# First pointwise layer by Strassen's scheme, with a ring of image blocks and a convolution by pairs of outputs

## The chip, the cores and the metric

The kernel runs on one core of a Trainium2 chip. The metric is the device time of one execution in microseconds (us). All arithmetic is fp32.

## What is computed

Two layers work on an image of 4 x 64 x 64 pixels with 256 channels. Layer 0 is full attention over the 4096 pixels of each image, added to its input. Layer 1 is a 3 x 3 depthwise convolution with three outputs per channel, two pointwise layers with a GELU between them, a residual, and attention over each pixel's 3 x 3 neighbours.

```python
# layer 0, x: (4, 4096, 256)
q, k, v = x @ Wq + bq, x @ Wk + bk, x @ Wv + bv        # q, k: 32 channels, v: 256
attn = softmax(einsum('bnd,bmd->bnm', q, k))
h = gamma * einsum('bnm,bmc->bnc', attn, v) + x
# layer 1
perceived = depthwise_conv3x3(h, w_perc) + b_perc       # 768 channels, zero padding
hid = gelu(einsum('bphw,dp->bdhw', perceived, w_up1) + b_up1)   # 768 -> 512
h_new = h + einsum('bdhw,cd->bchw', hid, w_up2) + b_up2         # 512 -> 256
q, k, v = split(einsum('bhwc,dc->bhwd', h_new, w_qkv) + b_qkv, 3)
w = softmax over 9 neighbours of (q . k_neighbour) / 16
return h_new + sum over 9 neighbours of w * v_neighbour
```

## The kernel before

Channels lie on the 128 partitions, in two halves of 128. The pixels of the four images are cut into 32 blocks of 512 pixels (8 rows). The main loop (L801) has one **slot** per block and a slot has 16 **points** (L800). In slot s the attention of layer 0 is computed for block s, and beside it layer 1 for earlier blocks: the convolution of block s-2, the two pointwise layers, scores and values of block k = s-3, and the result of the neighbour attention of block a = s-5. All orders are written out by hand: what a point issues goes to each engine's queue in that order, and each engine works through its queue in order.

At a point the kernel issues, in this order:

- at even points `energy` (L281): four matmuls that fill the four banks of tile `e` in PSUM for the next group of keys, and at every point `weight` (L293), the exponential on ScalarE of half of `e` into one of three `p` buffers;
- the jobs of that point, from the list at L807: `hidden` (L450, first pointwise layer, one of four output tiles of 128 channels), `update` (L475, second pointwise layer), `guide`, `scores`, `local_values` (L612), `local_product` (L741);
- `product` (L298): eight 512-column records on the two `acc` banks;
- `add_up` (L312), on VectorE, which sums the weights in `den`;
- some of the slot's convolution steps (`perceive`, L400): 48 steps spread evenly over 14 points. A step is one tap of one output tile of 128 x 512, `perc = window * weight + perc` on VectorE (L428). Tap 0 runs on ScalarE (L424). An output's eight steps follow one another before the next output's begin.

At the end of a slot, `partial_sums` and `finish` (L353) close the attention: a small matmul `dps` (L360), a reciprocal, a copy and a transpose, two scalings of the `acc` banks into `o` (L372), and two additions into the image `xp` in SBUF (L377), all on VectorE. GpSimd then adds every `o` into a watch tile (`watch`, L171, L176).

PSUM has eight banks: four for `e`, two tagged "acc", two tagged "m". All jobs and `dps` take the two "m" banks in turn (`job_bank`, L103), so a job's first matmul waits until whoever reads the result of the job two before it has done so.

`hidden(s, d)` multiplies six weight tiles of 128 x 128 by the six `perc` tiles of 512 columns into one bank, and ScalarE applies GELU with the bias out of the bank:

```python
for i in range(NPC):                                   # NPC = 6
    nc.tensor.matmul(ps, lhsT=wup1[:, i, bass.ts(d, P)], rhs=percs[s][i], ...)
nc.scalar.activation(hids[s][:, d, :], ps, AF.Gelu, bias=bup1[:, d : d + 1])
```

In the last slot of an image (slots 7, 15, 23) the queries, keys and values of the next image are projected (`fetch`, `project_qk`, `project_v`); in slot 0 those of blocks 3 to 7 of the first image are. `project_v` (L243) moves values out of PSUM on VectorE with an added bias. `xp` holds a whole padded image; `renew` (L113) brings its blocks over SP's DMA queue, the first image's eight at the start, later ones one per slot. SP's queue also carries the `ka`, `packed` and `qa` transfers and the outputs.

After the loop (from L897) a tail closes blocks 28 to 31. Its PSUM has six banks for jobs. Tail and last slot (L829) have job lists of their own; the last slot also runs most of the convolution of block 30.

Of the kernel before, what the change touches and what calls it, by code (L numbers as in the profile page):

```python
# [9 lines left out]
F32 = mybir.dt.float32  # L10
# [30 lines left out]
NSLOT = B * NBLK  # L41

# [8 lines left out]
def attention_then_perception_kernel(  # L51
# [34 lines left out]
    def unshifted():  # L86
# [23 lines left out]
        xp = pool.tile([P, CH, HP * WP], F32, tag="xp", name="xp")  # L110
        xv = xp.rearrange("p c (h w) -> p c h w", w=WP)

        def renew(slot, cs=slice(0, CH)):  # L113
            b, g = divmod(slot, NBLK)
            at = slice((1 + g * RB) * WP, (1 + (g + 1) * RB) * WP)
            nc.sync.dma_start(out=xp[:, cs, at], in_=x[b, :, cs, at])
# [8 lines left out]
        bv = loaded(b_v.partition_broadcast(P), "bv", [P, C], nc.scalar)  # L125
# [11 lines left out]
        for c in range(CH):  # L137
            nc.gpsimd.memset(xp[:, c, 0:WP], 0.0)
            nc.gpsimd.memset(xp[:, c, (HP - 1) * WP :], 0.0)
# [42 lines left out]
        def fetch(s):  # L182
# [18 lines left out]
            at = slice(1 + g * RB, 1 + (g + 1) * RB)  # L201
            for c in range(CH):
                to = staged[s][:, c, :].rearrange("p (h w) -> p h w", w=W)
                if b > 0:
                    nc.sync.dma_start(out=to, in_=rows[:, c, at, 1 : 1 + W])
                elif c == 0:
                    nc.vector.tensor_copy(to, xv[:, c, at, 1 : 1 + W])
                else:
                    nc.scalar.copy(to, xv[:, c, at, 1 : 1 + W])

        def project_qk(s):
# [17 lines left out]
            for r in range(2):  # L229
                at = 2 * r * CQK  # L230
                keys[s + r] = tile_of([P, P], "ka", f"ka_{s + r}", NBLK + 2)
# [11 lines left out]
        def project_v(s, pair, tag="m"):  # L243
# [4 lines left out]
            for i in range(2):  # L248
# [6 lines left out]
            nc.vector.tensor_tensor(  # L255
                values[s][:, 2 * pair : 2 * pair + 2, :],
                ps.rearrange("p (t c) -> p t c", c=C),
                bv.unsqueeze(1).to_broadcast([P, 2, C]),
                ALU.add,
# [93 lines left out]
        def finish(s, parts=((0, RB),)):  # L353

            g = s % NBLK
# [8 lines left out]
            rden = tile_of([P, NB], "rden", f"rden_{s}", 2)  # L364
            on_all(inverse[:, 0, :], turneds[s][:, 0, :], rden)
            watch(inverse.rearrange("p i j -> p (i j)")[:, :n])
            sums.pop(s)
            os = [tile_of([P, NB], "o", f"o_{s}_{c}", 3) for c in range(CH)]
            for r0, r1 in parts:
# [5 lines left out]
                for c, o in enumerate(os):  # L375
                    dst = xv[:, c, 1 + g * RB + r0 : 1 + g * RB + r1, 1 : 1 + W]
                    nc.vector.tensor_tensor(  # L377
                        dst, o[:, n].rearrange("p (h w) -> p h w", w=W), dst, ALU.add
                    )
                if len(parts) > 1:  # L380
                    yield
            for o in os:
                watch(o)
            yield

        def local_denominator(s):
            at = s + LAG_ATT - 1
            lrdens[s] = tile_of([P, NB], "rden", f"lrden_{s}", 2)
# [3 lines left out]
        percs, hids, hs = {}, {}, {}  # L392
        NPERC = NPC + 3
# [6 lines left out]
        def perceive(s, parts):  # L400

            g = s % NBLK
            ahead = s >= NSLOT - LAG_PERC
            percs.setdefault(s, {})

            def begin(i):
                if not ahead:
                    perc = tile_of([P, NB], "perc", f"perc_{s}_{i}", NPERC)
                else:
# [3 lines left out]
                    perc = percs[s, i - i % 2][:, i % 2, :]  # L413
                percs[s][i] = perc
                tap_of(i, 0, 0, RB)

            def tap_of(i, tap, r0, r1):
# [3 lines left out]
                win = xv[:, half, g * RB + dy + r0 : g * RB + dy + r1, dx : dx + W]  # L421
# [8 lines left out]
            for i, taps, r0, r1 in parts:  # L430
                if taps[0] == 0:
                    if i not in percs[s]:
                        begin(i)
                    if ahead and i + 1 < NPC:
                        begin(i + 1)
                for tap in taps:
                    if tap > 0:
                        tap_of(i, tap, r0, r1)
                        yield

        whole = [(i, range(TAPS), 0, RB) for i in range(NPC)]
# [3 lines left out]
            part for i in range(NPC)  # L445
            for part in ((i, range(LOW), 0, RB), (i, range(LOW, TAPS), 0, RB - 1))
        ]
        lower = [(i, range(LOW, TAPS), RB - 1, RB) for i in range(NPC)]
# [26 lines left out]
        def update(s, c):  # L475
            g = s % NBLK
# [8 lines left out]
            for half in range(2):  # L485
# [5 lines left out]
                    xv[:, c, 1 + g * RB : 1 + (g + 1) * RB, 1 + cols.start : 1 + cols.stop],  # L491
# [11 lines left out]
        def combine_steps():  # L503

            names, ws, turned = ("wq", "wk"), [], []
            for i, name in enumerate(names):
                w = tile_of([P, CH, C], "perc", f"{name}_in", NPERC)
# [3 lines left out]
            for name, w in zip(names, ws):  # L511
                t = tile_of([P, CH, C], "perc", f"{name}_turned", NPERC)
# [99 lines left out]
        def local_values(s, t):  # L612
# [8 lines left out]
            for half in range(2):  # L621
                if s < NSLOT - 2:
                    lvs[s, t, half] = tile_of([P, C], "lv", f"lv_{s}_{t}_{half}", 8)
                else:
                    if not half:
                        late[s, t] = tile_of([P, NB], "perc", f"lv_{s}_{t}", NPERC)
# [20 lines left out]
        def scores(s, half):  # L647
# [19 lines left out]
            else:  # L667

                if s < NSLOT:
                    late[s] = tile_of([P, NB], "perc", f"lp_{s}_{half}", NPERC)  # L670
# [61 lines left out]
        def local_reciprocal(s):  # L732
# [4 lines left out]
            lrdens[s] = tile_of([P, NB], "rden", f"lrden_{s}", 2)  # L737
# [3 lines left out]
        def local_product(s, c):  # L741
# [11 lines left out]
            o = tile_of([P, NB], "o", f"lo_{s}_{c}", 3)  # L753
# [22 lines left out]
        for i in range(4, NBLK):  # L776
            renew(i)
# [10 lines left out]
        gam = loaded(gamma.partition_broadcast(P), "gam", [P, 1])  # L788
        wlv = pool.tile([P, CH, C], F32, tag="wlv", name="wlv")
# [11 lines left out]
        for slot in range(NSLOT):  # L801
            b, g = divmod(slot, NBLK)
            if b > 0:
                renew(slot)
# [3 lines left out]
                job(hidden, k, 0) + job(hidden, k, 1), job(local_denominator, a),  # L808
                job(hidden, k, 2), job(local_product, a, 0), job(hidden, k, 3),
                job(local_product, a, 1), job(update, k, 0), job(update, k, 1), [],  # L810
                job(guide, k, 0), job(guide, k, 1), job(scores, k, 0),
                job(scores, k, 1) + job(local_sum, k - 1), job(local_values, k, 0),
                job(local_values, k, 1), [],
# [10 lines left out]
            conv = perceive(slot - LAG_PERC, whole) if slot >= LAG_PERC else iter(())  # L824
            n_steps, stepped = NPC * (TAPS - 1), 0
            if slot == NSLOT - 1:
# [3 lines left out]
                    job(hidden, k, 0) + job(hidden, k, 1), job(local_denominator, a),  # L830
                    job(hidden, k, 2), job(local_product, a, 0) + job(hidden, k, 3),
# [3 lines left out]
                    job(scores, k, 0) + job(hidden, k + 1, 0),  # L835
                    job(scores, k, 1) + job(local_sum, k - 1) + job(hidden, k + 1, 1),
                    job(hidden, k + 1, 2) + job(local_total, a + 1)
                    + job(local_reciprocal, a + 1),
                    job(hidden, k + 1, 3), job(update, k + 1, 0) + job(border, k),
# [6 lines left out]
            for point in range(points):  # L846
# [24 lines left out]
                while stepped < min(n_steps, -(-(point + 1) * n_steps // (points - 2))):  # L871
                    next(conv, None)
                    stepped += 1
                if slot == 0 and point == NG:
# [7 lines left out]
                    wup2 = loaded(w_up2, "wup2")  # L882
                    bup2 = loaded(b_up2, "bup2")
# [75 lines left out]
        return wv, bv, gam, wperc, bperc, wup1, bup1, wup2, bup2, blqk, blv  # L959


    def shifted():
# [16 lines left out]
        nc.scalar.dma_start(out=wqk, in_=w_qk)  # L979
        wqkv = own.tile([P, CH, 3 * C], F32, tag="wqkv", name="wqkv")  # L980
# [373 lines left out]
```

## Time and profile before

| quantity | value |
|---|---|
| median of 3 runs | 3572.64 us (3572.56 to 3573.12) |
| the profiled execution | 3573.02 us |
| its span, first to last instruction | 3571.3 us |
| TensorE busy | 3548.8 us (99%) |
| VectorE / ScalarE / GpSimd busy | 2320.2 / 1113.0 / 612.6 us |
| granted TensorE clock | 0.998 |
| first pointwise layer, L455 | 1536 matmul records, 686.8 us |
| convolution steps on VectorE, L428 | 1554, 1257.5 us |
| a slot without projections (2109.9 to 2215.8) | 105.9 us |

The profiled execution's time is the one that sums are made against; it lies 0.4 us over the median. PE stands for TensorE's matmuls, PEld for its weight loads, DVE for VectorE, ACT for ScalarE, POOL for GpSimd, SP for the engine whose queue issues most transfers. Each fp32 matmul appears as two records.

### The profile page before, as it was taken

Reading aid. Unit: us, or ns where it says so; the run is one execution under the profiler, and the core shown is the slowest. Engines: PE = TensorE matmul, PEld = TensorE weight load, DVE = VectorE, ACT = ScalarE, POOL = GpSimd, SP = SyncE. Lnnn points to the kernel's source line nnn. Section 1 sums busy time; section 2 is a strip of 40 time slices with the busy share of each in tenths; the row PEclk is TensorE's granted clock in tenths of the full one; section 3 lists DMA queues with packets and bytes.
Section 4 is the critical chain, followed back from the end, with each engine's and each line's share of the span. In section 5 each row is a group of like instructions: output and inputs, shape, how many; then the busy total and the mean of one; then the engine's idle time right before and its main releaser. Section 6 shows DMA issues by size and latency. Waiting matters only on the chain.

```text
span 3571.3 us, 29494 instructions
## 1 busy us (share of the span) xinstructions
PE 3548.8 (99%) x11346; PEld 1701.1 (48%) x11346; DVE 2320.2 (65%) x2938; ACT 1113.0 (31%) x1270; POOL 612.6 (17%) x804
## 2 busy tenths in 40 slices
PE   9999999999999999999999999999999999999998
PEld 4444444454444444455444444445544444444445
DVE  3386566657666666665666666665666666666875
ACT  2233333323333333322333333332233333333431
POOL 1000011111121121121111211111121122121123
PEclk9999999999999999999999999999999999999999
DMA  3000000110000000011000000001100000000000
GB/s 105 7 4 3 0 9 15 24 45 15 15 13 6 12 15 15 21 27 42 16 15 15 3 12 15 15 21 36 33 15 15 15 15 3 13 15 15 6 6 25
DMA packets 84533, 64.68 MB, mean 18 GB/s; under 512 B 57280, under 2 KB 62528, under 8 KB 84256
## 3 DMA queue, kind: packets, MB, share of 16 engines
q1 hardware_dynamic: 83568, 62.19, 6.2%
q8 instruction: 91, 1.49, 0.2%
q10 hardware_dynamic: 816, 0.53, 0.0%
q14 instruction: 58, 0.48, 0.0%
HBM read 41.52 MB, written 18.81 MB: 17 GB/s over the span
## 4 chain that ended last, share of the span: by engine, by line
PE 97%; DVE 2%; issue 0%; ACT 0%; DMA 0%; SPq 0%; ACTq 0%; DVEq 0%
PE acc L306 49%; PE hid L455 19%; PE e L287 8%; PE dx L481 6%; PE v L250 3%; PE lv L616 3%; PE g L564 3%; PE lo L747 3%; PE s L657 3%; DVE perc L428 2%; PE qk L216 1%; PE c L596 0%; DVE den L320 0%; PE ld L727 0%; PE dps L360 0%
## 5 line engine op out<-in xcount | busy, mean ns | idle before, releaser
L306 PE MATMUL acc<-p,v 128*128 128x512 f32 x4096 | 1834.2, 594 | 0.3 <-DVE o L372 0.3
L428 DVE SCALAR_TENSOR_TENSOR perc<-xp,wperc,perc 128x512 f32<-128x512 f32 (+1 forms) x1554 | 1257.5, 810 | 525.9 <-ACT perc L424 490.7
L306 PEld LDWEIGHTS acc<-p,v 128*128 128x128 f32 x4096 | 768.3, 190 | 916.0 <-issue 911.2
L295 ACT ACTIVATE p<-e 128x1024 f32<-128x1024 f32 x512 | 524.7, 1025 | 1467.2 <-PE e L287 835.2
L455 PE MATMUL hid<-perc,wup 128*128 128x512 f32 x1536 | 686.8, 600 | 0.0
L320 DVE TENSOR_TENSOR den<-den,p 128x1024 f32<-128x1024 f32 x480 | 594.8, 1239 | 42.8 <-ACT p L295 39.2
L455 PEld LDWEIGHTS hid<-perc,wup 128*128 128x128 f32 x1536 | 285.1, 190 | 389.7 <-issue 382.3
L176 POOL TENSOR_TENSOR watched<-watched,lo 128x256 f32<-128x256 f32 x124 | 157.0, 1266 | 999.0 <-DVE lo L754 994.0
L287 PE MATMUL e<-qa,ka 32*128 32x512 f32 x2048 | 291.9, 640 | 0.0
L481 PE MATMUL dx<-hid,wup 128*128 128x512 f32 x512 | 233.0, 598 | 0.0
L459 ACT ACTIVATE hid<-hid,bup 128x512 f32<-128x512 f32 x128 | 88.1, 688 | 436.3 <-PE hid L455 436.3
L629 DVE TENSOR_TENSOR lv<-lv,blv 128x256 f32<-128x256 f32 x130 | 49.1, 420 | 211.9 <-PE lv L616 211.9
L681 POOL TENSOR_TENSOR lp<-lp,near 128x396 f32<-128x396 f32 x60 | 57.7, 962 | 711.5 <-ACT lp L677 711.5
L487 DVE SCALAR_TENSOR_TENSOR h<-dx,bup,xp 128x256 f32<-128x256 f32 x128 | 56.0, 480 | 165.2 <-PE dx L481 165.2
L481 PEld LDWEIGHTS dx<-hid,wup 128*128 128x128 f32 x512 | 94.6, 190 | 129.9 <-issue 123.9
L424 ACT ACTIVATE perc<-xp,bperc,wperc 128x512 f32<-128x512 f32 x192 | 154.1, 804 | 5.2 <-PE hid L455 5.2
L295 ACT ACT_TABLE_LOAD x91 | 116.8, 1283 | 119.9 <-issue 119.3
L287 PEld LDWEIGHTS e<-qa,ka 32*128 32x128 f32 x2048 | 80.0, 182 | 148.0 <-issue 144.2
L176 POOL TENSOR_TENSOR watched<-watched,o 128x256 f32<-128x256 f32 x128 | 124.0, 969 | 56.2 <-DVE o L372 48.6
L616 PE MATMUL lv<-wlv,h 128*128 128x256 f32 x520 | 126.5, 385 | 1.4 <-DVE lv L629 0.7
L250 PE MATMUL v<-wv,xc 128*128 128x256 f32 x512 | 118.4, 384 | 6.3 <-DMA wv<-in_w_v 5.5
L564 PE MATMUL g<-h,wg 128*128 128x512 f32 x256 | 123.1, 604 | 0.0
(108 smaller groups left out, 1735.3 us busy)
## 6 DMA issues: line engine op xcount, KB each, us to landing
xp<-in_x SPq DMA_DIRECT2D x30, 528.0 KB, 4.2
out<-lo SPq DMA_DIRECT2D x58, 256.0 KB, 2.0
xc<-in_x SPq DMA_DIRECT2D x48, 256.0 KB, 3.4
qa<-packed SPq DMA_DIRECT2D x124, 64.0 KB, 2.1
ka<-st SPq DMA_DIRECT2D x124, 16.0 KB, 1.8
packed<-st SPq DMA_DIRECT2D x31, 64.0 KB, 1.9
wup<-in_w_up SPq DMA_DIRECT2D x1, 1536.0 KB, 7.0
out<-res SPq DMA_DIRECT2D x6, 256.0 KB, 2.0
```

The lines of the kernel that those rows point to most:

```text
L176: nc.gpsimd.tensor_tensor(at, at, values[:, i : min(n, i + C)], ALU.add)
L250: nc.tensor.matmul(ps[:, i * C : (i + 1) * C], lhsT=xc[:, kin, bass.ts(2 * pair + i, P)], rhs=wv[:, kin, :], start=(kin == 0), stop=(kin = ...
L287: nc.tensor.matmul(e[:, j, :], lhsT=key[rows, :], rhs=queries[s][rows, :], start=True, stop=True,)
L295: nc.scalar.activation(p, energies[s, G][:, 2 * half : 2 * half + 2, :], AF.Exp)
L306: nc.tensor.matmul(accs[s][c], lhsT=v[:, 2 * half + i, bass.ts(c, P)], rhs=p[:, i, :], start=(first and i == 0), stop=(G == NG - 1 and hal ...
L320: nc.vector.tensor_tensor(den, den, p, ALU.add)
L424: nc.scalar.activation(acc, win, AF.Identity, bias=bperc[:, half, j : j + 1], scale=wt)
L428: nc.vector.scalar_tensor_tensor(acc, win, wt, acc, ALU.mult, ALU.add)
L455: nc.tensor.matmul(ps, lhsT=wup1[:, i, bass.ts(d, P)], rhs=percs[s][i], start=(i == 0), stop=(i == NPC - 1),)
L481: nc.tensor.matmul(ps, lhsT=wup2[:, d, bass.ts(c, P)], rhs=hids[s][:, d, :], start=(d == 0), stop=(d == NHC - 1),)
L564: nc.tensor.matmul(ps, lhsT=wg[:, kin, bass.ts(i, P)], rhs=pixels(s, kin), start=(kin == 0), stop=(kin == CH - 1),)
L616: nc.tensor.matmul(ps[:, half * C : (half + 1) * C], lhsT=keys_of(s, t, half, kin), rhs=wlv[:, kin, :], start=(kin == 0), stop=(kin == CH ...
```

## The change

**Seven products.** Per block, the first pointwise layer is a product of a 512 x 768 weight matrix and a 768 x 512 matrix of convolution outputs. Both are cut in two in each direction, the columns into 256 and 256. The eight block products become seven. Weight combinations (`wmix`) are made once, on GpSimd. Sums of the convolution outputs are four additions of 128 x 256 for each of three tile pairs, run by VectorE as further steps of the convolution: 60 steps per block for 48. The products are then combined by VectorE out of PSUM into the SBUF tile `hid` (the first by a ScalarE copy), and GELU runs in place there. Blocks 30 and 31 keep the old form.

**Placement.** Two calls `hidden_part(k, d, part)` per output pair replace the four `hidden` calls, at points 0 to 3. `local_values(k-1, 1)` moves from point 14 to point 0 of the next slot, `local_product` from points 3 and 5 to 4 and 5.

**Pairs.** Convolution steps alternate between two outputs.

**Ring.** `xp` holds four blocks and two border rows, which `rim` fills. `renew` runs from slot 4, and blocks 4 to 7 are fetched for projection from memory by DMA and no longer by engine copies out of `xp`.

**Space.** The value bias is added to the image as gamma times bias, so that `project_v` becomes a ScalarE copy and the `xp` addition gets a third operand. `o` has two buffers for three, `ka` nine for ten, `lrden` one for two.

```diff
-        xp = pool.tile([P, CH, HP * WP], F32, tag="xp", name="xp")
+        RP = RING * RB + 2
+        xp = pool.tile([P, CH, RP * WP], F32, tag="xp", name="xp")
...
+            to, of = (slice(r * WP, (r + RB) * WP) for r in (ring(slot), 1 + g * RB))
+            nc.sync.dma_start(out=xp[:, cs, to], in_=x[b, :, cs, of])
...
-                if b > 0:
+                if s >= RING:
                     nc.sync.dma_start(out=to, in_=rows[:, c, at, 1 : 1 + W])
...
-            nc.vector.tensor_tensor(
-                values[s][:, 2 * pair : 2 * pair + 2, :],
-                ps.rearrange("p (t c) -> p t c", c=C),
-                bv.unsqueeze(1).to_broadcast([P, 2, C]),
-                ALU.add,
+            nc.scalar.copy(
+                values[s][:, 2 * pair : 2 * pair + 2, :], ps.rearrange("p (t c) -> p t c", c=C)
             )
...
-            rden = tile_of([P, NB], "rden", f"rden_{s}", 2)
+            rden = sums.pop(s)[:, 1, :]
...
-            os = [tile_of([P, NB], "o", f"o_{s}_{c}", 3) for c in range(CH)]
+            os = [tile_of([P, NB], "o", f"o_{s}_{c}", 2) for c in range(CH)]
...
-                    nc.vector.tensor_tensor(
-                        dst, o[:, n].rearrange("p (h w) -> p h w", w=W), dst, ALU.add
+                    nc.vector.scalar_tensor_tensor(
+                        dst, o[:, n].rearrange("p (h w) -> p h w", w=W), gbv[:, c : c + 1], dst,
+                        ALU.add, ALU.add,
                     )
...
+        def rim(s):
+            g = s % NBLK
+            if g == RING - 1:
+                nc.scalar.copy(xv[:, :, 0, :], xv[:, :, RP - 2, :])
+            elif g == NBLK - 1:
+                nc.gpsimd.memset(xv[:, :, 0, :], 0.0)
+            if g == RING:
+                nc.scalar.copy(xv[:, :, RP - 1, :], xv[:, :, 1, :])
+            elif (g == 0 and s > 0) or s == NSLOT - 2:
+                nc.gpsimd.memset(xv[:, :, RP - 1, :], 0.0)
...
+        def by_turns(outputs, taps, r0, r1):
+            return [(i, tap, r0, r1) for tap in taps for i in outputs]
+        MIXED = (
+            (MIX1, MIX3, UPPER2, ALU.add), (MIX3, LOWER, MIX3, ALU.subtract),
+            (MIX2, MIX1, LOWER, ALU.subtract), (MIX4, UPPER, MIX2, ALU.subtract),
+        )
+        mixed = [
+            step for j in range(MULT)
+            for step in by_turns((j, j + MULT), range(TAPS), 0, RB) + [(j, None, *m) for m in MIXED]
+        ]
...
+        def hidden_part(s, d, part):
...
+            def products(name, *todo):
+                ps = job_bank(f"hid_{s}_{d}_{name}")
+                for n, (w, kind) in enumerate(todo):
+                    for j in range(MULT):
+                        nc.tensor.matmul(
+                            ps[:, n * C : (n + 1) * C], lhsT=w(j), rhs=mixes[s, j][:, kind, :],
+                            start=(j == 0), stop=(j == MULT - 1),
+                        )
+                return ps.rearrange("p (a n) -> p a n", a=2)
...
+            if part == 0:
+                nc.scalar.copy(q[:, q22, :], products("a", (y11, LOWER))[:, 0, :])
+                bc = products("bc", (y21, UPPER), (t2, MIX2))
+                add(q[:, q11 : q22 + 1 : q22 - q11, :], bc, twice(q[:, q22, :]))
+            else:
+                de = products("de", (t3, MIX3), (t1, MIX1))
+                both = q[:, q21 : q12 + 1 : q12 - q21, :]
+                add(both, de, twice(q[:, q22, :]))
+                add(q[:, q22, :], q[:, q21, :], de[:, 1, :])
+                add(both, products("gf", (t4, UPPER2), (y22, MIX4)), both)
+                for i in (d, d + 2):
+                    nc.scalar.activation(
+                        hids[s][:, i, :], hids[s][:, i, :], AF.Gelu, bias=bup1[:, i : i + 1]
+                    )
...
-                job(hidden, k, 0) + job(hidden, k, 1), job(local_denominator, a),
-                job(hidden, k, 2), job(local_product, a, 0), job(hidden, k, 3),
-                job(local_product, a, 1), job(update, k, 0), job(update, k, 1), [],
+                job(local_values, k - 1, 1) + job(hidden_part, k, 0, 0),
+                job(local_denominator, a) + job(hidden_part, k, 0, 1),
+                job(hidden_part, k, 1, 0), job(hidden_part, k, 1, 1),
+                job(local_product, a, 0), job(local_product, a, 1),
+                job(update, k, 0), job(update, k, 1), [],
                 job(guide, k, 0), job(guide, k, 1), job(scores, k, 0),
-                job(scores, k, 1) + job(local_sum, k - 1), job(local_values, k, 0),
-                job(local_values, k, 1), [],
+                job(scores, k, 1) + job(local_sum, k - 1), job(local_values, k, 0), [], [],
...
+                to = min(n_steps, -(-(point + 1) * n_steps // (points - 2)))
+                if point < 3:
+                    to = min(to, n_mixed // MULT)
```

## The prediction

> **What bounds the kernel now.** I read the busy table first, then the chain of work that ended last, then that chain in order of time over one slot, then VectorE in order of time at the same place.
>
> ```profile
> PE 3548.8 (99%) x11346; PEld 1701.1 (48%) x11346; DVE 2320.2 (65%) x2938; ACT 1113.0 (31%) x1270; POOL 612.6 (17%) x804
> ...
> PE 97%; DVE 2%; issue 0%; ACT 0%; DMA 0%; SPq 0%; ACTq 0%; DVEq 0%
> ```
>
> TensorE is the bound: 99% busy and 97% of the chain. A shorter PE list is worth its full length as long as no new wait opens in it. The waits view of PE between 250 and 3300 us is empty. The chain in order of time (start us, us, what) gives the prices:
>
> ```profile
> 2205.76 1.93 PE lv L616 x8
> ...
> 2214.55 0.14 PE dps L360 x2
> 2214.69 1.07 PE e L287 x8
> 2215.76 10.50 PE hid L455 x24
> 2226.26 6.87 PE acc L306 x16
> 2233.12 1.07 PE e L287 x8
> 2234.20 5.35 PE hid L455 x12
> ...
> 1563.58 3.45 PE v L250 x16
> ```
>
> An fp32 matmul is two records. A 512-column record takes 6.87/16 = 0.429 us, a 256-column one 3.45/16 = 0.2157 us. A group behind `e` takes 0.2 us more, whatever it is (5.35 against 12 x 0.429 = 5.15). The group table's means (600 and 384 ns) contain overlap and are not the pace. VectorE where a slot begins (start, us, line, operation):
>
> ```profile
> 2214.73 0.36 DVE L363 RECIPROCAL inverse<-dps 128x32 f32<-128x32 f32 x1 [1.59 <-PE dps L360]
> 2215.12 0.43 DVE L348 COPY turned<-inverse 128x512 f32<-128x512 f32 x1
> 2215.58 0.71 DVE L351 STREAM_TRANSPOSE rden<-turned 128x512 f32<-128x512 f32 x1
> 2216.33 1.41 DVE L372 SCALAR_TENSOR_TENSOR o<-acc,gam,rden 128x512 f32<-128x512 f32 x2
> 2217.66 1.98 DVE L377 TENSOR_TENSOR xp<-o,xp 128x512 f32<-128x512 f32 x2
> 2219.56 1.21 DVE L317 COPY den<-p 128x1024 f32<-128x1024 f32 x1
> ```
>
> With T0 = 2214.55, the start of `dps`, VectorE is tied up by `finish` until T0+5.01. Today 10.5 us of `hid` hide that.
>
> **What the Trainium skill says.** (1) "TensorE: Matmul & The Clock Gate", Back-to-back issue gap: N/2.4 + 2.5 ns. Its estimate for two passes is 432 ns at N = 512 and 218 ns at 256; the trace has 429 and 216, so halving the columns is nearly free. (2) "SBUF — State Buffer", Who interferes with whom: a DVE instruction with two SBUF inputs contends with a GpSimd one that reads SBUF. The trace agrees: the two L377 adds take 1.98 us beside `watch(o)` on POOL, while a 128x512 add with one SBUF input is 692 ns. (3) "VectorE: DVE Perf Modes", The DRAIN you can't avoid: the next operation doesn't start until the pipe is empty, but one that isn't held starts earlier. In the trace two independent `lv` adds of 418 ns take 0.76 us together (0.34 apart), while dependent convolution steps of 752 ns start 0.785 apart.
>
> **The change, part by part.**
> *Seven products for eight.* A slot's hidden layer was 48 records x 0.429 = 20.6 us. It becomes 7 products x 2 output tiles x 3 matmuls x 2 records = 84 x 0.2157 = 18.1 us. There is one 0.2 us surcharge per `e` before and after. The gain is 2.5 us, for blocks 0 to 29 (30 and 31 keep the old form): **-75.0 us**. A weight load (190 ns) still fits under 216 ns, as it does in `v`. Bounds: 0.2145 to 0.22 a record, -78 to -64.
>
> *The wait it adds.* Point 0 now holds `local_values(k-1,1)`, then products a and bc. `job_bank` has two "m" banks: dps takes one, lv the other, a the first, bc the second. So bc waits until VectorE has read lv, and those adds are queued behind `finish`. PE: `dps`+`e` end at T0+1.21, lv (1.93, as at 2205.76) T0+3.14, a (6 x 0.216) T0+4.43. VectorE: free at T0+5.01, two lv adds 0.76, T0+5.77. Wait 1.34; the `xp` add becomes a three-operand form (744 to 752 ns against 692), 2 x 0.05 more: 1.45 us. Behind bc on PE are product(0,0) and everything else, so it counts fully. Slots 4 to 31 have an lv there: 28 x 1.45 = **+40.6 us**. Bounds: the adds at an uncontended 0.75 each give 0.85 (+24); at 1.65, the worst that a contended convolution step shows in the chain view of the last slot, 2.7 (+76).
>
> *The other bank waits.* I walk on from bc's end at T0+8.4. VectorE: bc's add 0.69 (like L255) to 9.1, `den` copy and add 2.6, five convolution steps to about 15.5, `local_denominator` 1.1, then de's adds (0.69+0.42) at 17.7 and gf's at 18.4. PE: product to 11.8, de to 14.4, gf to 17.0, product to 20.4, `e` to 21.5. The next a needs de's bank (17.7) and the next bc needs gf's (18.4): 3.8 us to spare, and likewise at point 2 to 4. Taken at 0. If that cover went, each point would add its lateness. GELU follows gf's add by about 2.5 us and `update` is two points later.
>
> *VectorE and ScalarE load.* Per slot VectorE gets 12 mixes of about 0.35 to 0.42 and two sets of 0.69 x 3 + 0.42, about +9.5 us; pairs make neighbouring steps independent, 48 x about 0.1 = -5 (bounds 0 to -5.5). That is 71 us (slot 2109.9 to 2215.8) to about 75 of 103: hidden. ScalarE takes the value evictions (64 x about 0.62, as its copy L209), and copies of a, but loses a pair of 1283 ns table loads per slot: 31%, hidden. The rim copies wait for `finish` in two slots of eight; behind them exp(1,0) and the copy of a end near T0+7, before bc's end. Hidden.
>
> *Ring, queues.* `renew` on SP waits for slot-1's convolution and `update`, done at the slot's start, and is needed a slot later: 0. In slot 0 the blocks 4 to 7 come by DMA (3.4 us to landing) instead of by engine copies. On SP they stand behind the `ka` and `packed` issues (0.6 us each, to about 41 us for the second pair) and two small loads, and project_qk at 32.6 and 47.5 us wants them at once: 0 to 4 us, **+1.5**. The key ring of nine tiles still has a free tile when each key pair is written: 0.
>
> *Last slot.* It runs 126 steps instead of 114, nine per point, with `update` in the first points. VectorE was already the chain there (3319 to 3378). A point of VectorE is then 9 x 0.67 + 1.2 (`den`) + about 0.8 (a `lo`, `h` or `lv` operation) = 8 us, one of PE about 8.2, and the 16 steps of point 3, held until gf frees the tile, put VectorE about 6 us behind. So `local_values` waits for the `h` writes (0.7 us), then for the bank of the lv before it (1.5), and `border` for the next (1.1): **+3** (0 to 7).
>
> *Tail.* Pairs save about 0.1 on some 16 steps that bind: **-1.5**. `o` has two buffers for three, so the last product's outputs wait for POOL's watch and add and the DMA of block 30: the second add ends at 3561.48, issue and 2.0 us landing give 3563.5, where that write stood at 3561.95: **+1.6**.
>
> Sum: -75.0 + 40.6 + 1.5 + 3 - 1.5 + 1.6 = -29.8. The profiled execution took 3573.0 us (span 3571.3 and 1.7 around it); the median of the runs is 0.4 less. 3573.0 - 29.8 - 0.4 = **3543 us**. About 0.2% (7 us) is what a measurement of this kernel can tell from no change.
>
> **Rivals.**
> *A, the wait at bc is hidden.* The bank freed earlier, or quicker `xp` adds. For: nothing waits in PE there today. Against: 5.01 of `finish` is in the trace and two banks are two banks. Only the gain and the small terms (1.5 + 3 - 1.5 + 1.6 = 4.6): 3572.6 - 75.0 + 4.6 = 3502 us; with half the wait, 3522.
>
> *B, slower: the same place at a higher price.* The two three-operand `xp` adds run into POOL's four watch operations (4.13 us in a row from T0+2.7) with the lv adds behind them. The gain of 75 is used up once the wait reaches about 2.5 us a slot (28 x 2.5 + 4.6 = 75). If `xp` adds take 1.65 and 1.65 plus a late start, 3.0 us: 84 + 4.6 - 75 = +14, 3586 us. For: contended convolution steps did reach 1.65. Against: in the slots that I looked at, the two adds take 1.98 to 1.99 under the same POOL operations.
>
> *C, VectorE falls behind in points 1 to 4 too.* If pairs save nothing and mixes collide with POOL, a bank handover or two costs about 0.6 us a slot more: 3543 + 18 = 3561. Against: 3.8 us of room.
>
> *D, the products aren't faster.* If a 256-column record cost 0.235 on alternating weights and slices, the gain would be 26 us and the result about 3592. Against: `v` and `lv` in this trace run at 0.216.
>
> **How the numbers follow.** Forecast, 3530 to 3556: 0.56. A, 3499 to 3525: 0.17. C: 0.10. B 0.10 and D 0.03, slower; 0.04 between, within 0.2%. Faster by over 0.2%: 0.56 + 0.17 + 0.10 = 0.83; same 0.04; slower 0.13. The range reaches from A's lower half to C's upper end, 3505 to 3567, leaving out B, D and a few of A, under 2 in 10.
>
> **What would show it.** Right: groups of 12 `hid` records at 2.6 us; slots near 104.6 us for 105.7; one PE wait of about 1.45 us at bc, released by the lv add, in 28 slots, none at a, de, gf; convolution steps 0.67 to 0.70 apart. The sum is wrong if bc's wait is absent or over 2.5 us, if records of 256 exceed 0.22, or if `e` begins to wait for ScalarE.

## The result and the profile after

| quantity | before | after |
|---|---|---|
| median of 4 runs each | 3572.6 us (3572.25 to 3573.12) | 3549.98 us (3548.67 to 3551.44) |
| ratio to before, 95% interval | | 0.9937 (0.9919 to 0.9954) |
| the profiled execution / its span | 3573.02 / 3571.3 us | 3551.44 / 3549.7 us |
| a slot without projections (two of eight are 0.24 us longer) | 105.66 us | 104.83 us |

The kernel became faster by 22.6 us. Forecast were 29.6 less, 3543 us; the time lies 7 us over that and inside the range.

The busy table and the engine shares of the chain, after:

```profile
PE 3483.7 (98%) x12426; PEld 1903.1 (54%) x12426; DVE 2463.6 (69%) x3471; ACT 1084.7 (31%) x1336; POOL 628.9 (18%) x815
...
PE 92%; DVE 6%; issue 1%; DMA 0%; SPq 0%; POOL 0%; ACT 0%; ACTq 0%; DVEq 0%; POOLq 0%
```

TensorE lost 65 us of busy time, but the execution only 22. The chain says where the rest went: VectorE's share rose from 2% to 6%. (PE works beside most of that stretch; only the wait at its end costs time.) The waits of PE between 250 and 3200 us (us in total, times, longest), empty before, have exactly one line:

```profile
PE hid_bc L527 <- DVE lv L735: 37.1, 27, 1.4
```

With the one in the last slot there are 28, of 1.37 us each. The chain in order of time (start us, us, what) where a slot begins:

```profile
2093.68 0.15 PE dps L361 x2
...
2095.46 0.04 DVE o L373
2095.50 0.63 issue
2096.13 0.74 DVE o L373
2096.87 1.90 DVE xp L378 x2
2098.77 0.67 DVE lv L735 x2
2099.44 0.04 issue
2099.49 2.86 PE hid_bc L527 x12
2102.34 3.43 PE acc L308 x8
2105.78 2.59 PE hid_de L527 x12
2108.37 2.59 PE hid_gf L527 x12
...
2115.46 1.49 PE hid_a L527 x6
2116.95 2.59 PE hid_bc L527 x12
```

The chain leaves PE at `dps`, runs through `finish` on VectorE and the two `lv` adds, and returns to PE at `bc`: the path that the prediction walked. (The "issue" of 0.63 is only the overlap of the two scalings.) A group of 12 records takes 2.59 us as forecast, but the chain puts 2.86 on the `bc` behind the wait. PE in order of time shows what these 0.27 us are:

```profile
2096.65 1.46 PE L527 MATMUL hid_a<-perc,wup 128*128 128x256 f32 x6
2099.49 1.56 PE L527 MATMUL hid_bc<-perc,wup 128*128 128x256 f32 x6 [1.38 <-DVE lv L735]
2100.89 1.46 PE L527 MATMUL hid_bc<-perc,wmix 128*128 128x256 f32 x6
2102.18 3.60 PE L308 MATMUL acc<-p,v 128*128 128x512 f32 x8
```

Six records show as 1.46 us, but in an unbroken stream the next group starts after 1.29 (2100.89 to 2102.18). Without a wait `bc` would so have started at 2097.95. It starts 1.54 us later, and the wait line counts only 1.37 of them, from the end of `a` as the view draws it. The first six records of `bc` then take 1.40 instead of 1.29. So a wait of 1.37 in the view costs 1.64.

VectorE in order of time (start, us, line, operation, idle before) over the same stretch:

```profile
2096.78 1.98 DVE L378 SCALAR_TENSOR_TENSOR xp<-o,gbv,xp 128x512 f32<-128x512 f32 x2
2098.69 0.74 DVE L735 TENSOR_TENSOR lv<-lv,blv 128x256 f32<-128x256 f32 x2
2102.45 0.69 DVE L534 TENSOR_TENSOR hid<-hid_bc,hid 128x512 f32<-128x512 f32 x1 [3.02 <-PE hid_bc L527]
...
2104.92 3.40 DVE L463 SCALAR_TENSOR_TENSOR perc<-xp,wperc,perc 128x512 f32<-128x512 f32 x5
...
2110.01 0.42 DVE L534 TENSOR_TENSOR hid<-hid,hid_de 128x256 f32<-128x256 f32 x1
2111.00 0.69 DVE L534 TENSOR_TENSOR hid<-hid_gf,hid 128x512 f32<-128x512 f32 x1 [0.56 <-PE hid_gf L527]
```

With T0 = 2093.68, de's adds end at T0+16.8 and gf's at T0+18.0 (walked: 17.7 and 18.4), and nothing waits at a, de or gf. The two three-operand `xp` adds take 1.98 us, as the two-operand ones did. Five convolution steps take 3.40 us, so they start 0.67 apart, for 0.785 before.

From the starts of all `dps` groups in both traces I get the length of every slot, and from these the ledger of the whole execution:

| stretch | before | after | difference | what it is made of |
|---|---|---|---|---|
| start to the end of slot 0 | 112.11 | 114.58 | +2.47 | project_qk waits for blocks that come by DMA (but see below) |
| slots 1 and 2 | 135.54 | 135.53 | 0 | |
| slot 3 | 102.24 | 98.05 | -4.19 | -2.47 products, -1.72 a `local_values` job moved to slot 4 |
| slots 4 to 30 | 2956.7 | 2934.3 | -22.4 | 27 x (-2.47 products, +1.64 wait) |
| last slot | 141.30 | 145.84 | +4.54 | -4.94 products of two blocks, +1.64 wait, +1.73 moved job, +6.1 other |
| tail | 123.42 | 121.38 | -2.04 | |
| span | 3571.3 | 3549.7 | -21.6 | |

The 1.64 is what is left over: a slot fell by 0.83 where the products alone give 2.47 (a value that the first experiment confirms). It is 1.37 of wait and the 0.27 that the wait line leaves out.

The first row rests on one pair of traces. Seven of the kernels below leave slot 0 as it is after the change, and in their traces it ends between 112.70 and 114.21; one leaves it as before and ends at 112.84. Over these ten traces the mean difference is +1.3.

### The profile page after: what moved, and what is told of

Read it like the earlier page. It is cut to its first block, busy times and chain, and to the rows that moved or that the text cites. A ratio compares the mean times of both kernels' runs of the same rounds, so it can differ in the third digit from the quotient of the medians.

```text
span 3549.7 us, 32536 instructions
## 1 busy us (share of the span) xinstructions
PE 3483.7 (98%) x12426; PEld 1903.1 (54%) x12426; DVE 2463.6 (69%) x3471; ACT 1084.7 (31%) x1336; POOL 628.9 (18%) x815
## 3 DMA queue, kind: packets, MB, share of 16 engines
q8 instruction: 100, 1.64, 0.2%
## 4 chain that ended last, share of the span: by engine, by line
PE 92%; DVE 6%; issue 1%; DMA 0%; SPq 0%; POOL 0%; ACT 0%; ACTq 0%; DVEq 0%; POOLq 0%
PE acc L308 49%; PE e L289 7%; PE dx L584 6%; PE hid_bc L527 5%; PE hid_de L527 4%; PE hid_gf L527 4%; PE g L670 3%; PE v L255 3%; PE lo L853 3%; PE s L763 2%; PE lv L722 2%; DVE xp L378 1%; DVE perc L463 1%; PE hid_a L527 1%; PE hid L559 1%; PE qk L221 1%
## 5 line engine op out<-in xcount | busy, mean ns | idle before, releaser
L463 DVE SCALAR_TENSOR_TENSOR perc<-xp,wperc,perc 128x512 f32<-128x512 f32 (+2 forms) x1554 | 1159.3, 805 | 64.9 <-ACT perc L459 64.9
L322 DVE TENSOR_TENSOR den<-den,p 128x1024 f32<-128x1024 f32 x480 | 586.1, 1221 | 104.0 <-ACT p L297 102.3
L787 POOL TENSOR_TENSOR lp<-lp,near 128x396 f32<-128x396 f32 x60 | 87.2, 1453 | 678.3 <-ACT lp L783 678.3
L534 DVE TENSOR_TENSOR hid<-hid_bc,hid 128x512 f32<-128x512 f32 x60 | 41.5, 691 | 219.9 <-PE hid_bc L527 219.9
L469 DVE TENSOR_TENSOR perc<-perc 128x256 f32<-128x256 f32 x360 | 171.6, 490 | 7.2
L527 PE MATMUL hid_de<-perc,wmix 128*128 128x256 f32 x720 | 165.2, 379 | 0.0
L527 PEld LDWEIGHTS hid_de<-perc,wmix 128*128 128x128 f32 x720 | 136.8, 190 | 43.7 <-issue 28.2
L459 ACT ACTIVATE perc<-xp,bperc,wperc 128x512 f32<-128x512 f32 x192 | 145.2, 806 | 0.0
L527 PE MATMUL hid_bc<-perc,wup 128*128 128x256 f32 x360 | 90.5, 387 | 41.3 <-DVE lv L735 38.5
L722 PEld LDWEIGHTS lv<-wlv,h 128*128 128x128 f32 x520 | 96.1, 190 | 53.8 <-issue 35.2
```

What stands on the lines that cost most here:

```text
L322: nc.vector.tensor_tensor(den, den, p, ALU.add)
L459: nc.scalar.activation(acc, win, AF.Identity, bias=bperc[:, half, j : j + 1], scale=wt)
L463: nc.vector.scalar_tensor_tensor(acc, win, wt, acc, ALU.mult, ALU.add)
L469: nc.vector.tensor_tensor(t[:, to, :], t[:, a, :], t[:, b, :], op)
L527: nc.tensor.matmul(ps[:, n * C : (n + 1) * C], lhsT=w(j), rhs=mixes[s, j][:, kind, :], start=(j == 0), stop=(j == MULT - 1),)
L722: nc.tensor.matmul(ps[:, half * C : (half + 1) * C], lhsT=keys_of(s, t, half, kin), rhs=wlv[:, kin, :], start=(kin == 0), stop=(kin == CH ...
```

## The experiments

My theory: the wait at `bc` costs 1.64 us in 28 slots, it comes from the bank of the moved `lv` job behind `finish`, and it eats 46 of the 74 us. Rivals: the products themselves are worth less than 2.47, or another cost of the change (combinations on VectorE, pairs, ring, rim) uses up the difference. Every kernel was timed beside fresh runs of the kernel before, whose medians were 3572.1 to 3572.5; the ratios are to these.

### The second local_values job back at point 14

```diff
-                job(local_values, k - 1, 1) + job(hidden_part, k, 0, 0),
+                job(hidden_part, k, 0, 0),
...
-                job(scores, k, 1) + job(local_sum, k - 1), job(local_values, k, 0), [], [],
+                job(scores, k, 1) + job(local_sum, k - 1), job(local_values, k, 0),
+                job(local_values, k, 1), [],
```

Expected: 

> The changed kernel with the second local_values job back at point 14 of its own slot; nothing else differs. Theory (bank wait): the two m banks are then dps and a, and bc gets the bank that dps left, which VectorE has read 0.4 us after dps. The wait of 1.37 us and the 0.27 us of restart at bc go in 28 slots: 46 us less, 3504 us (3498 to 3510), and no PE wait between 250 and 3200 us. Rival (finish itself is in the way): product needs the acc banks, which finish holds, so the wait only moves from bc to product: 3535 us or more.

Measured: 3506.48 us (3504.76 to 3509.13), ratio 0.9819 (0.9804 to 0.9834). The slots are 103.19 us, which is 105.66 - 2.47, and no wait of PE is left between 250 and 3200 us. The chain in order of time at the same place:

```profile
2067.70 0.14 PE dps L361 x2
2067.84 1.07 PE e L289 x8
2068.91 1.49 PE hid_a L527 x6
2070.41 2.59 PE hid_bc L527 x12
2073.00 3.43 PE acc L308 x8
```

PE goes from `dps` through to `bc` with no detour, and `bc` takes 2.59 again. The products are worth their whole price, and the combinations, pairs, ring and rim cost nothing in these slots.

### The order a, bc, lv at point 0

```diff
-                job(local_values, k - 1, 1) + job(hidden_part, k, 0, 0),
+                job(hidden_part, k, 0, 0) + job(local_values, k - 1, 1),
```

Expected: 

> The changed kernel with the two jobs of point 0 in the other order: a and bc first, then local_values. Theory (bank wait): bc gets the bank of dps and lv the bank of a, which ScalarE has copied; nothing in front of product waits for VectorE's queue behind finish. 46 us less, 3504 us (3498 to 3512). Rival (finish itself is in the way): as before the wait appears at product or at the next job, 3535 us or more. A second rival (VectorE's load is too high): no change, 3550.

Measured: 3520.26 us (3518.57 to 3520.75), ratio 0.9853 (0.9838 to 0.9868). A miss. All slots are as long as in the first experiment except eight, which are 1.64 us longer: in each image those for which `rim` copies a border row. The one line in PE's waits from 250 to 3200 us, and ScalarE in order of time in such a slot:

```profile
PE lv L722 <- ACT hid L540: 11.1, 8, 1.4
```

```profile
2078.79 0.30 ACT L395 COPY xp<-xp 128x132 f32<-128x132 f32 x1 [7.50 <-DVE xp L378]
2079.00 1.02 ACT L297 ACTIVATE p<-e 128x1024 f32<-128x1024 f32 x1
2079.92 0.36 ACT L540 COPY hid<-hid_a 128x256 f32<-128x256 f32 x1
```

`lv` now takes the bank of `a`. Its reader, the copy of `a`, stands on ScalarE behind the rim copy, which waits for `finish`, and behind an exponential. It ends at 2080.28, T0+6.8, about where the prediction put it ("near T0+7"); in the kernel after, the wait at `bc` covers that, and here nothing does. 8 x 1.64 = 13.1 of the 13.8 us between this kernel and the last.

### The same with the rim copies on GpSimd

```diff
-                nc.scalar.copy(xv[:, :, 0, :], xv[:, :, RP - 2, :])
+                nc.gpsimd.tensor_copy(xv[:, :, 0, :], xv[:, :, RP - 2, :])
...
-                nc.scalar.copy(xv[:, :, RP - 1, :], xv[:, :, 1, :])
+                nc.gpsimd.tensor_copy(xv[:, :, RP - 1, :], xv[:, :, 1, :])
```

Expected: 

> The kernel with the order a, bc, lv at point 0, and the two rim copies moved from ScalarE to GpSimd. Theory, in that kernel the 8 slots of 104.83 us come from the copy of a, which stands on ScalarE behind the rim copy and the exp: with the rim copies on GpSimd all slots fall to 103.19 us, PE waits for no copy of a, 3520.3 less 8 x 1.64 is 3507 us (3503 to 3510). Rival, exp(1,0) alone or another wait of these slots holds the copy of a: the 8 slots stay above 104 us, 3515 to 3521 us.

Measured: 3506.37 us (3504.58 to 3507.24), ratio 0.9814 (0.9801 to 0.9828). All the slots are as long as in the first experiment, and PE waits for nothing between 250 and 3200. The rim copy on ScalarE was the whole of the miss.

### GpSimd's watch of o issued two points later

```diff
             if s < NSLOT - 1:
                 rim(s)
+                yield
             for o in os:
                 watch(o)
...
+                if point == 2 and slot > 0:
+                    next(closing)
```

Expected: 

> The changed kernel with the four GpSimd watch operations on o issued at point 2 of the next slot instead of beside the two additions into xp. Theory (contention sets the price of the wait): the two xp additions take about 1.45 us instead of 1.90, so lv is read 0.45 us sooner and the wait at bc falls from 1.37 to about 0.9 us in 28 slots: 13 us less, 3537 us. Rival (the additions are that slow by themselves): the wait stays at 1.37, 3550 us.

Measured: 3552.32 us (3548.93 to 3554.8), ratio 0.9942 (0.9928 to 0.9955). GpSimd in order of time shows why this tells nothing:

```profile
2095.92 3.81 POOL L181 TENSOR_TENSOR watched<-watched,o 128x256 f32<-128x256 f32 x4 [1.57 <-DVE o L373]
```

The four operations still start as soon as `o` is written. Being issued later didn't delay them: GpSimd stood idle for 1.57 us before them, so they waited only for their own inputs. The claim stayed untested, and the next kernel takes the operations out.

### No watch of o in the slots

```diff
-            for o in os:
-                watch(o)
+            if s == NSLOT - 1:
+                for o in os:
+                    watch(o)
```

Expected: 

> The kernel after, without GpSimd's four watch operations on o in slots 0 to 30 (the range watch on the first product's outputs is left out of the kernel; the last slot keeps it). Theory, contention: the two xp adds start 0.4 us after GpSimd begins these operations and take 1.98 us each beside them; alone they take about 1.45 and overlap, so that the lv adds start 0.5 to 0.6 us earlier, the wait of TensorE at bc falls from 1.37 to about 0.8 us and the time to 3535 us (3531 to 3540). Rival, the xp adds are slow by themselves (two PSUM-free three-operand adds at 1.98): wait and time unchanged, 3550 us.

Measured: 3534.68 us (3532.71 to 3536.23), ratio 0.9896 (0.9881 to 0.9911). VectorE in order of time, and PE's waits:

```profile
2085.65 1.41 DVE L378 SCALAR_TENSOR_TENSOR xp<-o,gbv,xp 128x512 f32<-128x512 f32 x2
2086.98 0.75 DVE L736 TENSOR_TENSOR lv<-lv,blv 128x256 f32<-128x256 f32 x2
```

```profile
PE hid_bc L528 <- DVE lv L736: 21.6, 27, 0.8
```

The adds take 1.41 us for 1.98 and the wait falls by the same 0.57, to 0.80. So 16 of the 46 us are the collision of two engines, and 30 are the order of the queue. The slots are 104.26 us, 1.07 above those without a wait: again the wait and the 0.27.

### The pairs alone, in the kernel before

```diff
-        whole = [(i, range(TAPS), 0, RB) for i in range(NPC)]
+        def by_turns(outputs, taps, r0, r1):
+            return [(i, tap, r0, r1) for tap in taps for i in outputs]
+        pairs = [(i, i + 1) for i in range(0, NPC, 2)]
+        whole = [step for p in pairs for step in by_turns(p, range(TAPS), 0, RB)]
```

(The lists for block 30 in the last slot are made the same way, with its third output not begun before point 3.)

Expected: 

> The kernel before with the convolution by pairs of outputs alone (in the last slot the third output is not begun before point 3). Theory (VectorE is off the path outside the last slot and the tail): convolution steps 0.67 us apart instead of 0.785, VectorE's busy time down by 100 to 170 us, and the time 0 to 4 us less, 3570 us. Rival (VectorE's load does set the pace): at least 10 us less, 3562 us or under.

Measured: 3569.74 us (3569.45 to 3570.4), ratio 0.9993 (0.9985 to 1.0001). The steps start 0.67 to 0.69 apart, VectorE's busy time falls by 62 us and not by 100 or more, no slot from 4 to 30 changes, and the time falls by 2.7 us. VectorE has room in a slot, so a faster convolution buys nothing there. What it gains is in the tail, which takes 119.62 us for 123.41.

### One output at a time, in the kernel after

```diff
-            return [(i, tap, r0, r1) for tap in taps for i in outputs]
+            return [(i, tap, r0, r1) for i in outputs for tap in taps]
```

Expected: 

> The kernel after, with the convolution one output at a time again (steps 0.785 us apart in place of 0.67). Theory: in slots 4 to 30 the convolution stands in VectorE's idle time, so the slots stay at 104.83 us and the wait at bc at 1.37; only the last slot, where VectorE is the chain, gets later by 3 to 12 us: 3553 to 3562 us. Rival, the pairs keep VectorE in time at points 1 to 4: without them slots of over 105.4 us and waits at de or gf, 3570 us or more.

Measured: 3553.31 us (3553.15 to 3556.57), ratio 0.9949 (0.9935 to 0.9963). The slots stay at 104.83 and the wait at 1.37, which settles the question that was asked. The 3 us are behind the slots. The last slot grows from 145.84 to 148.71, but PE's waits in it add up to less than in the kernel after (7.7 us against 8.2). The clock differs: it reads 1.00 all through that slot in the kernel after, and here 0.83 from 3330 to 3340 and again from 3380 to 3390, which is up to 3.4 us lost. So it isn't shown that the steps cost anything in the last slot. The tail grows from 121.38 to 124.52 (see the tail, in the section on the prediction).

### Blocks 4 to 7 fetched ahead

```diff
         fetch(3)
+        for i in range(4, NBLK):
+            fetch(i)
...
         def early(s):
-            fetch(s)
-            fetch(s + 1)
             project_qk(s)
```

Expected: 

> The kernel after, with the staging of blocks 4 to 7 issued straight after that of blocks 0 to 3, ahead of the first projection's ka and packed DMAs on SP. Theory, the start's 2.5 us are the SP queue (the xc DMAs stand behind ka and packed issues): qk of blocks 4 and 6 wait no longer, slot 0 is shorter by 2.3 to 2.5 us, everything later moves by as much, 3547.5 us. Rival, the DMA itself or contention with the loads of weights: slot 0 unchanged or later, 3550 to 3552 us.

Measured: 3552.9 us (3549.38 to 3555.8), ratio 0.9945 (0.9931 to 0.9959): nothing gained. The trace shows half of the theory. The waits of `qk` for `xc` are gone. But `dps` of slot 0 starts at 113.28, no earlier than in kernels that leave slot 0 alone (112.70 to 114.58), since a new wait of 2.8 us stands before the third `e`: two small loads (gam and gbv) had gone behind the new DMAs on SP, VectorE's queue stood on them until 37.0 us, with it the sums that free the `p` buffers, and so the exponential. The last slot took 149.59 us for 145.84 besides, with the clock at half for 10.2 us of it (see the clock, below).

### The last slot paced

```diff
+                elif slot == NSLOT - 1:
+                    to = min(n_steps, (30, 39, 48, 56, 64)[point - 3] if point < 8 else 64 + 9 * (point - 7))
```

Expected: 

> The kernel after, with the convolution steps of the last slot that are held until point 3 spread over points 3 to 7 (12, 9, 9, 8, 9) in place of 18 at once at point 3. Theory, the burst puts VectorE behind so that lv, bc and ld wait in the last slot: these waits (about 6 us) fall by half, the last slot goes from 145.8 to about 143 us, 3547 us (3545 to 3549). Rival, VectorE has too much to do in the last slot as a whole: the waits only move to later points, 3549 to 3552 us.

Measured: 3546.86 us (3545.57 to 3547.68), ratio 0.9928 (0.9914 to 0.9941). First VectorE and then PE's waits from 3280 us, of the kernel after:

```profile
3320.51 12.63 DVE L463 SCALAR_TENSOR_TENSOR perc<-xp,wperc,perc 128x512 f32<-128x512 f32 x16
...
3342.39 8.01 DVE L463 SCALAR_TENSOR_TENSOR perc<-xp,wperc,perc 128x512 f32<-128x512 f32 x9
3350.32 0.74 DVE L735 TENSOR_TENSOR lv<-lv,blv 128x256 f32<-128x256 f32 x2
...
3358.93 5.91 DVE L463 SCALAR_TENSOR_TENSOR perc<-xp,wperc,perc 128x512 f32<-128x512 f32 x9
```

```profile
PE lv L722 <- DVE lv L735: 3.1, 1, 3.1
PE hid_bc L527 <- DVE lturned L841: 2.8, 1, 2.8
```

The 16 steps of point 3 keep VectorE busy for 12.6 us, and the `lv` adds come 3.1 us late. With the steps spread over points 3 to 7 the same view has:

```profile
PE hid_bc L527 <- DVE lturned L841: 2.2, 1, 2.2
...
PE lv L722 <- DVE lv L735: 0.4, 1, 0.4
```

and the last slot has 142.99 us. PE's waits in it fall by half, from 8.2 us to 3.9, as the theory said; the slot gains only 2.85 of these 4.3, since the clock went to half for 3.4 us, which cost 1.7 (see the clock, below). Most of what is left is the other wait: `bc` behind the reciprocal of the neighbour attention, itself behind nine more steps on VectorE.

The steps themselves are dearer in the burst: nine take 8.01 us before the `lv` adds and 5.91 later. The first three of the 8.01 run beside GpSimd's watch of `lo` and its addition to `lo`, and take 1.22, 1.22 and 1.75 us each for 0.74:

```profile
3341.42 2.77 POOL L181 TENSOR_TENSOR watched<-watched,lo 128x256 f32<-128x256 f32 x2 [17.44 <-DVE lo L860]
3344.27 1.60 POOL L870 TENSOR_TENSOR lo<-lo,h 128x512 f32<-128x512 f32 x1
```

It is the same picture as at the `xp` additions, but no run took these operations out.

### All that helped together

The first experiment, the pacing and the early fetch in one kernel, with the two small loads ahead of the fetch:

```diff
+        gam = loaded(gamma.partition_broadcast(P), "gam", [P, 1])
+        gbv = loaded(b_v.rearrange("o (c p) -> p (o c)", p=P), "gbv")
+        for i in range(4, NBLK):
+            fetch(i)
```

Expected: 

> The kernel with the second local_values job back at point 14, the last slot's convolution paced over points 3 to 7, the staging of blocks 4 to 7 issued ahead of the first projections and the two small loads gam and gbv issued ahead of that. Theory, the three add up: 3506.5 (second job at point 14) less 2.9 (pacing, 145.84 to 142.99 in the last slot) less about 2 (slot 0, with neither the qk waits nor the wait for exp behind gbv) is 3501.5 us (3498 to 3505); the main slots 103.19 us, the first dps at 111 to 112 us, the last slot about 140.3. Rival, the last slot's waits were set by the moved job and not by the burst: the pacing adds nothing there, 3504 to 3507 us.

Measured: 3496.93 us (3496.01 to 3498.08), ratio 0.9789 (0.9776 to 0.9803), 1 us below the range of the forecast, the fastest kernel here and 53 us ahead of the kernel after. The slots are 103.19 us, the last one 139.62, which is the 142.99 of the paced kernel less 1.64 for the wait and 1.73 for the moved job; the clock stood at half for 3.4 us in both. `dps` of slot 0 starts at 109.52, better than forecast and than before (112.11): the waits for `xc`, both those for the DMA and those that before had for the copies on VectorE and ScalarE, are gone. Part of it is a quicker start: the first `qk` group took 1.94 us here, 2.14 in the kernel before and 3.04 in the kernel after.

### What the clock adds in the last slot

Runs of the kernels with a wait of 3.1 us in the last slot spread over 2.2 to 6.4 us, those of before, which waits 0.7 us at most in it, over 0.9 to 2.2. Between the start and the last wait of the kernel, the traces have the clock below full only in the last slot and the tail: at half, for 3.4 or 6.8 us at a time. The `lv` group behind the wait of 3.1 us, in the kernel after and in the one that fetches ahead, both with the same order there:

```profile
3351.12 1.99 PE L722 MATMUL lv<-wlv,h 128*128 128x256 f32 x8 [3.11 <-DVE lv L735]
```

```profile
3349.79 3.78 PE L722 MATMUL lv<-wlv,h 128*128 128x256 f32 x8 [3.11 <-DVE lv L735]
```

The same eight records take twice as long. The stretch from 3350 to 3360 us, with the granted clock third from last, in the same two kernels:

```profile
3350.00:3360.00 10.00, 8.88 (x39) 4.73 (x40) 9.90 (x18) 1.27 (x3) 0.80 (x1) 1.00 0.00 0
```

```profile
3350.00:3360.00 10.00, 10.00 (x29) 5.42 (x29) 9.90 (x17) 0.69 (x1) 0.00 (x0) 0.72 0.00 0
```

The Trainium skill, "TensorE: Matmul & The Clock Gate", Part 1, says that the array falls to half clock after an idle window of about 3.4 us, and that the window runs freely, so that where the clock changes varies from run to run. Half clock and the variation agree. The length does only roughly: here a wait of 3.1 us was enough in one trace and not in the other, and in the paced kernel six records took 2.77 us for 1.46, and the clock read 0.66 in a stretch of 5 us, just after a wait of 2.15. The waits of 1.37, one in a slot of 105 us, never lowered it: it reads 1.00 in every stretch of 10 us up to 3000. But shorter waits that lay close together stand before a half clock in the tails: in the kernel after, waits of 0.44 and 1.25 us end at 3473.3 and 3478.5, and from 3479.4 the clock is at half for 3.4 us. So no single length is shown to be the limit. That it was the wait that lowered it is argued from the order in time; no run took it apart.

## Why the prediction was right, and where its sizes were off

| step | predicted | measured |
|---|---|---|
| seven products, 30 blocks | -75.0 | -74.1 (2.47 a block) |
| wait at bc, 28 slots | +40.6 (1.45) | +45.9 (1.64) |
| other bank waits in the slots | 0 | 0 |
| slot 0 | +1.5 | +2.5 (+1.3 over ten traces) |
| last slot | +3 | +6.1 |
| tail | +0.1 | -2.0 |
| sum | -29.8 | -21.6 |

**Right in mechanism.** The price of a 256-column record, the place of the wait, its releaser, its number and the room at the other banks held. Rival A (no wait) and rival D (dearer records) are refuted by the one wait line and by the 2.59 us groups, C by the absence of waits at a, de and gf. The seven products were summed with 2.5 us a block where 84 and 48 records give 2.47; that is all of their 0.9 us. B named the right place; its price of 2.5 us was not reached, since the three-operand `xp` adds took 1.98 as the old ones did.

**The wait** is the largest miss. Its length was nearly right (1.34 before the dearer adds, 1.37 measured), and the 0.1 for the third operand was not needed. What failed is "1.45 us": I counted only the time that the view shows as idle, and not the 0.27 us that a wait costs besides, where the record before it no longer overlaps the one behind it and the first record behind it is slower. Two kernels with waits of 1.37 and 0.80 and one with none give 1.64, 1.07 and 0. The part in it that the collision with GpSimd makes is 0.57 us.

**The last slot.** The mechanism was right (VectorE the chain, the burst of point 3, waits of `lv`), the size half of it. I saw three waits of 0.7, 1.5 and 1.1. Those for the `h` writes were 0.4 and 0.5, the one for the bank of `lv` was 3.1, `border` didn't wait, and one of 2.8 at `bc` behind the reciprocal I didn't see. The "126 steps" was also wrong: 18 of them never run there, so it is 108 for 96. Nine steps a point was right all the same, but not always their 0.67 us: beside GpSimd's additions nine took 8.01, which is 0.89 each.

**The tail.** The wait for an `o` buffer that I priced at 1.6 is in the trace: the last product's outputs wait 1.9 us for the DMA of block 30, and PE's last wait grows from 3.08 to 4.76. The tail became shorter all the same, because the -1.5 for the pairs was too small. Two experiments measured it: the pairs alone shorten the tail of the kernel before by 3.8 us, and without them that of the kernel after is longer by 3.1. How much of both is the clock, for which I had no term, stays open. Up to the last wait of the kernel it stands at half for 6.8 us in the tail of the kernel before and not at all with the pairs alone, for 3.4 us in the kernel after and for 6.8 without the pairs. But two kernels with the pairs and no half clock in the tail (no watch of `o`; rim copies on GpSimd) are only 0.6 and 0.4 us shorter there than the kernel after. The 3.8 less and the 1.7 more of the last wait make up the -2.0.

**What cancelled.** The terms were 10.3 us too low in all and 2.1 too high in the tail. The sum misses by 8.2 and would miss by 10.3 had the tail been right, so a fifth of the misses cancelled by luck.

**Costed at nothing.** The combinations and pairs on VectorE, and the value evictions on ScalarE, cost nothing in the slots, as said. The rim copies cost nothing only while the wait at `bc` covers them: without that cover they cost 13 us, and the prediction named the cover but not this price.

## What to carry to other kernels

Leaving out one of eight block products in one layer was worth its full 74 us, and a job that could have stayed where it was (the second `lv`, put between `dps` and the products) took 46 of them back. When a change reorders jobs on a pool of two banks, walk each bank to its reader, and ask which long sequence that reader stands behind on its engine. Before a cover is removed, look at what else it covers: the wait at `bc` hid a copy on ScalarE.

## What the runs showed of the hardware

- A wait of TensorE cost 0.27 us more than the idle time in the view, at waits of 0.80 and 1.37 alike: 0.17 that the record before it no longer overlaps the next, and 0.10 in the group behind it (2.69 us from its start to the next group's for 2.59).
- Two three-operand 128x512 adds from SBUF take 1.98 us together beside GpSimd's adds from SBUF, and 1.41 where these are left out; the two-operand form took 1.98 beside them too. This agrees with what the prediction cites of "SBUF — State Buffer".
- Convolution steps of 752 ns start 0.67 us apart when neighbours are independent and 0.785 when each needs the one before.
- After a wait of about 3 us TensorE sometimes ran the next group at half pace (3.78 for 1.99 us). The half clock lasted 3.4 or 6.8 us at a time, and in the tails it came behind waits of 1.5 us and less too.
